# The tail of a two-layer graph kernel: scores of the last group between its value products, an early count of the reciprocals, and three residual adds on GpSimd

## The chip, the cores and the metric

The kernel runs on one core of a Trainium2 chip. The metric is the device time of one launch in microseconds (us), the median of several runs. PE is TensorE, DVE is VectorE, ACT is ScalarE, POOL is GpSimd, SP is SyncE, which issues the writes to memory.

Runs of the same kernel differ by more than the effects studied here: the part of the program ahead of the change took between 1581.35 and 1582.98 us in the profiles below (e4 apart, which changes that part). So, beside the medians, I read from each profile the **tail**: from the start of the scores of batch 123 (the first work that the change touches in earnest) to the end of the instruction that writes the flag.

## The reference, cut to what matters

```python
# layer 0: x is (128 batches, 128 nodes, 512 features)
h = relu(layernorm(x))
x = x + max_over_features(relu(adj @ h + b))           # becomes one number c per batch and node
# layer 1
h = relu(layernorm(x))
q, k, v = h @ Wq + bq, h @ Wk + bk, h @ Wv + bv        # 8 heads of 64
w = softmax(q k^T / 8 + mask(adj == 0))
x = x + w v
```

The softmax is computed without subtracting a maximum: exponentials, times a 0/1 mask, and the row sums come out of the value product through a column of ones in v. At the end the kernel counts how many reciprocals of sums lie in a sane range; if not all do, a general and slower version runs behind it.

## The kernel before

Batches go in groups of four. The products q, k, v of the next group (seven products of eight matmuls each, `p1` to `p7`, for each of q, k, v) are spread over the four batches of the present group, so that TensorE has work while the masks and scalings of a batch run on the other engines. The last group has no next group: only the last product of its own v (`p3`) is left to fill in.

```python
work  = ctx.enter_context(tc.tile_pool(name="work", bufs=2))       # w and o: two buffers each
ps_sc = ctx.enter_context(tc.tile_pool(name="ps_sc", bufs=1, space=PSUM))
ps_av = ctx.enter_context(tc.tile_pool(name="ps_av", bufs=1, space=PSUM))
# ... cut ...
def scores(g, i):          # 16 matmuls over 64 partitions, then two exponentials on ACT
def masks(w):              # two DVE products, both inputs in SBUF
def finish(g, i, w):
    pav = ps_av.tile([P, 2, 512], F32, name="pav")
    # ... 32 matmuls w^T v into 64 partitions each: the "value product" ...
    nc.vector.reciprocal(rs, po[:, :, :, HD])
    o = work.tile([P, 2, 4, HD], F32, name="o")
    nc.vector.tensor_tensor(o, po[:, :, :, 0:HD], rs..., op=ALU.mult)        # scaling, from PSUM
    nc.vector.scalar_tensor_tensor(y, X[g][:, i, :], C[g][:, i : i + 1], y,  # residual
                                   op0=ALU.add, op1=ALU.add)                 # (y is o)
    nc.sync.dma_start(out[b], y)
# ... cut ...
for b in range(B):
    w = scores(g, i)
    for s in range(max(5, len(parts[i]))):
        if s < len(parts[i]):
            parts[i][s]()                  # one product of the next group
        if s == 0:
            masks(w)
        # ... cut: normalisation of later batches ...
    finish(g, i, w)
# behind the loop: two DVE passes over all 1024 reciprocals, a matmul with ones, the flag
```

## Time and profile before

| | before |
|---|---|
| median of 3 runs | 1621.87 us (1621.35 to 1623.84) |
| span of the profile | 1620.0 us |
| start of batch 123's scores to the flag | 1617.21 - 1581.78 = 35.43 us |
| last residual's end to the flag's end | 1617.21 - 1614.91 = 2.30 us |
| flag to the end of the span | 2.79 us |

The prediction below shows the views. The way to read them: the page says which engine bounds the whole (TensorE), and hence that only stretches in which TensorE idles can be shortened by moving other work. The stretches say where those are. The chain says what TensorE waits for there.

### The profile page before, as it was taken

What the parts mean: (1) busy time and instruction counts of PE and PEld (TensorE: products, weight loads), DVE (VectorE), ACT (ScalarE), POOL (GpSimd) and SP (SyncE); (2) the same over time, 40 slices, a digit from 0 to 9 for tenths busy, and PEclk for the clock granted to TensorE, in tenths of its full rate; (3) what the DMA queues carried; (4) which work ended last, traced back from release to release, by engine and by line L of the source; (5) the groups of instructions that cost most, each with busy time, mean ns of one, the idle gap of its engine ahead of it and who ended that gap; (6) DMA issues with size and microseconds to landing.
All of it is one profiled execution on the core that took longest, in us unless ns stands there. A gap on an engine that the chain in (4) does not pass through costs nothing.

```text
span 1620.0 us, 29469 instructions
## 1 busy us (share of the span) xinstructions
PE 1586.6 (98%) x11819; PEld 1319.8 (81%) x11819; DVE 1114.2 (69%) x2044; ACT 422.9 (26%) x844; POOL 259.6 (16%) x278
## 2 busy tenths in 40 slices
PE   6899999999999999999999999999999999999996
PEld 4688888888888888888888888888888888888885
DVE  3576777766777767777767777667777677777655
ACT  2322222222222222222222222222222222222221
POOL 4311111111111111111111111111111111111000
PEclk9999999999999999999999999999999999999999
DMA  4033222232222232222332222322222322223201
GB/s 164 1 72 73 68 60 51 69 75 69 63 46 70 69 79 65 67 44 69 72 73 68 54 56 69 76 68 64 47 69 69 79 65 67 44 69 73 47 27 40
DMA packets 299082, 104.02 MB, mean 64 GB/s; under 512 B 264448, under 2 KB 264576, under 8 KB 298944
## 3 DMA queue, kind: packets, MB, share of 16 engines
q1 hardware_dynamic: 297520, 99.69, 25.5%
q8 instruction: 94, 1.54, 0.4%
q10 hardware_dynamic: 1248, 2.16, 0.4%
q14 instruction: 44, 0.36, 0.1%
q0 software_dynamic: 176, 0.27, 0.1%
HBM read 37.03 MB, written 33.55 MB: 44 GB/s over the span
## 4 chain that ended last, share of the span: by engine, by line
PE 97%; DVE 1%; ACT 1%; issue 0%; DMA 0%; POOL 0%; ACTq 0%; DVEq 0%; POOLq 0%
PE mm L372 72%; PE pav L499 9%; PE sc L477 8%; PE mm L306 6%; PE mm L445 1%; PE pav L306 1%; PE sc L299 0%; DVE w L490 0%; DMA xg<-in_x_dram 0%; ACT hn L272 0%; DVE o L512 0%; DVE o L508 0%; POOL rstd L264 0%; DVE st L259 0%; ACT qT L450 0%
## 5 line engine op out<-in xcount | busy, mean ns | idle before, releaser
L264 POOL TENSOR_TENSOR rstd<-ve,mhalf 128x1 f32<-128x1 f32 x128 | 84.3, 659 | 1225.9 <-DVE ve L262 1087.6
L485 ACT ACTIVATE w<-sc 128x512 f32<-128x512 f32 x256 | 138.9, 595 | 515.4 <-PE sc L477 515.4
L499 PEld LDWEIGHTS pav<-v,w 128*64 128x64 f32 x4096 | 130.3, 137 | 99.6 <-issue 54.4
L372 PE MATMUL mm<-hs,sq_sb 128*128 128x256 f32 x744 | 179.0, 383 | 0.0
L372 PE MATMUL mm<-hs,sk_sb 128*128 128x256 f32 x768 | 176.4, 379 | 0.0
L372 PE MATMUL mm<-sv_sb,hs 128*128 128x256 f32 x768 | 176.2, 379 | 0.0
L273 POOL TENSOR_TENSOR xg<-xg,bv_sb 128x512 f32<-128x512 f32 x128 | 162.9, 1273 | 35.2 <-DVE hn L269 27.5
L490 DVE TENSOR_TENSOR w<-w,live 128x512 f32<-128x512 f32 x256 | 164.7, 685 | 1.0 <-ACT w L485 1.0
L372 PEld LDWEIGHTS mm<-sv_sb,hs 128*128 128x128 f32 x768 | 145.9, 190 | 20.7 <-issue 1.0
L272 ACT ACTIVATE hn<-hn,rstd 128x512 f32<-128x512 f32 x128 | 92.9, 726 | 267.7 <-DVE hn L269 206.3
L372 PEld LDWEIGHTS mm<-hs,sk_sb 128*128 128x128 f32 x768 | 145.9, 190 | 20.3 <-issue 0.5
L372 PEld LDWEIGHTS mm<-hs,sq_sb 128*128 128x128 f32 x744 | 138.8, 190 | 21.4
L499 PE MATMUL pav<-v,w 128*64 128x65 f32 x4096 | 148.5, 224 | 6.7 <-DVE w L490 6.7
L477 PE MATMUL sc<-qT,kT 64*128 64x128 f32 x2048 | 148.7, 285 | 0.0
L420 DVE TENSOR_TENSOR u<-mm,p1b 128x512 f32<-128x512 f32 x63 | 43.5, 691 | 128.3 <-PE mm L372 128.3
L477 PEld LDWEIGHTS sc<-qT,kT 64*128 64x128 f32 x2048 | 124.2, 187 | 9.1 <-issue 0.3
L372 PE MATMUL mm<-hT,wk_sb 128*128 128x256 f32 x512 | 124.2, 385 | 0.0
L372 PE MATMUL mm<-wv_sb,hT 128*128 128x256 f32 x512 | 120.9, 379 | 0.0
L306 PE MATMUL mm<-hn,adjT 128*128 128x512 f32 x236 | 120.5, 592 | 0.0
L372 PE MATMUL mm<-hT,wq_sb 128*128 128x256 f32 x496 | 120.4, 386 | 0.0
L372 PEld LDWEIGHTS mm<-wv_sb,hT 128*128 128x128 f32 x512 | 97.3, 190 | 13.7 <-issue 0.5
L372 PEld LDWEIGHTS mm<-hT,wk_sb 128*128 128x128 f32 x512 | 94.7, 190 | 15.8 <-issue 0.5
(84 smaller groups left out, 2033.1 us busy)
## 6 DMA issues: line engine op xcount, KB each, us to landing
out_dram<-o SPq DMA_DIRECT2D x128, 256.0 KB, 2.1
xg<-in_x_dram SPq DMA_DIRECT2D x62, 512.0 KB, 5.1
hT<-tb SPq DMA_DIRECT2D x960, 32.0 KB, 2.0
xg<-in_x_dram SPq DMA_DIRECT2D x2, 256.0 KB, 3.4
xg<-in_x_dram ACTq DMA_DIRECT2D x2, 256.0 KB, 5.6
wq_sb<-in_L_gnn_Wq_dram SPq DMA_DIRECT2D x1, 512.0 KB, 7.9
wk_sb<-in_L_gnn_Wk_dram SPq DMA_DIRECT2D x1, 512.0 KB, 11.1
wq_sb<-in_L_gnn_Wq_dram ACTq DMA_DIRECT2D x1, 512.0 KB, 10.6
```

The costliest lines, as they stand in the source:

```text
L264: nc.gpsimd.tensor_tensor(rstd, ve, mhalf, op=ALU.pow)
L272: nc.scalar.activation(HN[m], HN[m], AF.Copy, scale=RSTD[m])
L273: nc.gpsimd.tensor_tensor(X[g][:, i, :], X[g][:, i, :], bv_sb, op=ALU.add)
L306: nc.tensor.matmul(pa, adjT, HN[m], start=True, stop=True)
L372: nc.tensor.matmul(bank[:, r, :], lhs, rhs, start=first and r == 0 and c == 0, stop=r == 1 and c == 1, skip_group_check=True,)
L420: nc.vector.tensor_tensor(self.u3, self.b, self.pf[1], op=ALU.add)
L445: nc.tensor.matmul(bank[:, r, :], W["q"][:, c, k * P : (k + 1) * P], h[:, :, c], start=r == 0 and c == 0, stop=r == 1 and c == NC - 1, ski ...
L477: nc.tensor.matmul(psc[:, j, f, :], KT[g][r, f, i * D : (i + 1) * D], QT[g][r, f, i * D : (i + 1) * D], start=True, stop=True,)
L485: nc.scalar.activation(w[:, j], psc[:, j], AF.Exp, scale=HD ** -0.5)
L490: nc.vector.tensor_tensor(w[:, j], w[:, j], live_h, op=ALU.mult)
L499: nc.tensor.matmul(pav[r, h // 4, (h % 4) * HE : (h % 4 + 1) * HE], w[:, h % 2, h // 2, r], V[g % 2][:, i, h, :], start=True, stop=True,)
```

## The change

Its intent is to keep TensorE fed in the last group. The v of the last group is built during batch 123 anyhow; the new order puts the scores of batches 124 to 127 between those products, so that exponentials and masks run early. Two spare places for the weights are the idle `tb` tiles; one value product goes to the idle score bank. The count is split, and three residuals leave DVE: ACT adds c to x, GpSimd adds the result to the scaled output.

```diff
+def spare_tile():
+    t = proj.tile([P, NQ, 2, NC, Q], F32, name="tb")
+    return t.rearrange("p a i c r -> p (a i c r)")
 # ... cut: scores(g, i, spare=False): with spare, its weights go to a tb tile ...
-def finish(g, i, w):
+def finish(g, i, w, spare=False, eng=nc.vector):
     # ... cut: with spare, the value product goes to ps_sc ...
-    nc.vector.scalar_tensor_tensor(y, X[g][:, i, :], C[g][:, i : i + 1], y, op0=ALU.add, op1=ALU.add)
+    if eng is nc.vector:
+        eng.scalar_tensor_tensor(y, x_b, c_b, y, op0=ALU.add, op1=ALU.add)
+    else:
+        nc.scalar.activation(x_b, x_b, AF.Identity, bias=c_b)
+        eng.tensor_tensor(y, x_b, y, op=ALU.add)
-for b in range(B):
+for b in range(B - G - 1):
     # ... cut ...
+        elif s == 3 and b == B - 2 * G + 1:
+            count(0, B - 2 * G)
 # ... cut: the whole count at the end removed ...
+w = scores(g - 1, G - 1)
+k3()
+masks(w)
+v6()
+w0 = scores(g, 0)
+v2()
+masks(w0)
+finish(g - 1, G - 1, w)
+v7()
+w1 = scores(g, 1)
+v5()
+masks(w1)
+w2 = scores(g, 2, spare=True)
+v4()
+masks(w2)
+w3 = scores(g, 3, spare=True)
+finish(g, 0, w0, eng=nc.gpsimd)
+PR[g][2].p3()
+masks(w3)
+finish(g, 1, w1, eng=nc.gpsimd)
+finish(g, 2, w2, spare=True, eng=nc.gpsimd)
+finish(g, 3, w3)
+count(B - 2 * G, B)
```

More of the change, by code (lines that the diff above doesn't have):

```diff
@@ L208, in fast @@
         ps_av = ctx.enter_context(tc.tile_pool(name="ps_av", bufs=1, space=PSUM))
+        CNT = []
         X, HN, TB, HT, HB, QT, KT, C, AMAX, WA, RSTD, MV, PR = ({} for _ in range(13))
@@ L469, in products, with scores @@
             )
-        def scores(g, i):
+        def spare_tile():
+            t = proj.tile([P, NQ, 2, NC, Q], F32, name="tb")
+            return t.rearrange("p a i c r -> p (a i c r)")
+        def scores(g, i, spare=False):
             psc = ps_sc.tile([P, 2, NC, D], F32, name="sc")
@@ L482, in scores @@
                     )
-            w = work.tile([P, 2, NC, D], F32, name="w")
+            if spare:
+                w = spare_tile().rearrange("p (j f d) -> p j f d", j=2, f=NC)
+            else:
+                w = work.tile([P, 2, NC, D], F32, name="w")
             for j in range(2):
@@ L490, in masks @@
                 nc.vector.tensor_tensor(w[:, j], w[:, j], live_h, op=ALU.mult)
-        def finish(g, i, w):
+        def finish(g, i, w, spare=False, eng=nc.vector):
             b = g * G + i
-            pav = ps_av.tile([P, 2, 512], F32, name="pav")
+            if spare:
+                pav = ps_sc.tile([P, 2, NC, D], F32, name="sc").rearrange("p j f d -> p j (f d)")
+            else:
+                pav = ps_av.tile([P, 2, 512], F32, name="pav")
             for h in range(H):
@@ L511, in finish, with count @@
             y = o.rearrange("p k h d -> p (k h d)")
+            x_b, c_b = X[g][:, i, :], C[g][:, i : i + 1]
+            if eng is nc.vector:
+                eng.scalar_tensor_tensor(y, x_b, c_b, y, op0=ALU.add, op1=ALU.add)
+            else:
+                nc.scalar.activation(x_b, x_b, AF.Identity, bias=c_b)
+                eng.tensor_tensor(y, x_b, y, op=ALU.add)
+            nc.sync.dma_start(out[b], y)
+        def count(b0, b1):
+            r = RS[:, b0:b1].rearrange("p b h -> p (b h)")
+            ok = (spare_tile() if b0 == 0 else live)[:, 0 : (b1 - b0) * H]
+            cnt = const.tile([P, 1], F32, name=f"cnt{len(CNT)}")
+            CNT.append(cnt)
+            nc.vector.tensor_single_scalar(ok, r, SUM_LO, op=ALU.is_ge)
             nc.vector.scalar_tensor_tensor(
-                y, X[g][:, i, :], C[g][:, i : i + 1], y, op0=ALU.add, op1=ALU.add
+                ok, r, SUM_HI, ok, op0=ALU.is_le, op1=ALU.mult, accum_out=cnt
             )
-            nc.sync.dma_start(out[b], y)
         with tc.manual_schedule():
@@ L582, in fast @@
                     move(m)
-            ok = work.tile([P, 2, NC, D], F32, name="w").rearrange("p j f d -> p (j f d)")
-            cnt = stat.tile([P, 1], F32, name="cnt")
-            rs_all = RS.rearrange("p b h -> p (b h)")
-            nc.vector.tensor_single_scalar(ok, rs_all, SUM_LO, op=ALU.is_ge)
-            nc.vector.scalar_tensor_tensor(
-                ok, rs_all, SUM_HI, ok, op0=ALU.is_le, op1=ALU.mult, accum_out=cnt
-            )
+            g = NG - 1
+            k3, v6, v2, v7, v5, v4 = parts[G - 1]
+            w = scores(g - 1, G - 1)
[21 more added lines that the diff above has]
+            count(B - 2 * G, B)
             pc = ps_mm.tile([P, 512], F32, name="mm")
-            nc.tensor.matmul(pc[0:1, 0:1], cnt, ones, start=True, stop=True)
+            for k in range(2):
+                nc.tensor.matmul(pc[0:1, 0:1], CNT[k], ones, start=k == 0, stop=k == 1)
             nc.vector.tensor_copy(flag, pc[0:1, 0:1])
```

## The prediction

> **What bounds the kernel now.** I read the page first (engine shares, slices, chain of waits), then the stretches of the last 40 us, the chain piece by piece, the waits and the transfers.
>
> ```profile
> span 1620.0 us, 29469 instructions
> PE 1586.6 (98%) x11819; PEld 1319.8 (81%) x11819; DVE 1114.2 (69%) x2044; ACT 422.9 (26%) x844; POOL 259.6 (16%) x278
> PE 97%; DVE 1%; ACT 1%; issue 0%; DMA 0%; POOL 0%; ACTq 0%; DVEq 0%; POOLq 0%
> ```
>
> TensorE (PE) is busy 98% of the span and holds 97% of the chain. Until the last group it does not wait, so nothing moved off VectorE (DVE) there gains anything. Only the end is open. The stretches (busy us of PE, PEld, DVE, ACT, POOL, each with a count):
>
> ```profile
> 1581.85:1593.49 11.64, 11.64 (x66) 10.00 (x68) 5.52 (x9) 1.67 (x3) 0.00 (x0) 1.00 0.06 24
> 1593.49:1597.63 4.14, 4.10 (x57) 3.36 (x56) 2.34 (x4) 1.08 (x2) 0.00 (x0) 1.00 0.08 32
> 1597.63:1613.12 15.49, 8.77 (x176) 7.41 (x176) 10.52 (x18) 3.26 (x6) 0.00 (x0) 1.00 0.16 61
> 1613.12:1617.21 4.09, 0.19 (x2) 0.09 (x2) 3.63 (x7) 0.00 (x0) 0.00 (x0) 0.52 0.17 64
> 1617.21:1620.00 2.79, 0.00 (x0) 0.00 (x0) 0.00 (x0) 0.00 (x0) 0.00 (x0) 0.50 0.03 9
> ```
>
> Up to 1597.63 PE is full. Then come four batches in which it works 8.77 of 15.49 us, a close of 4.09 us on DVE, and 2.79 us of branch and shutdown. One of those batches in the chain (start, length, what):
>
> ```profile
> 1603.73 1.06 PE pav L499 x28
> 1604.79 0.02 issue
> 1604.82 0.22 DVE RS L506
> 1605.04 0.02 issue
> 1605.06 0.70 DVE o L508
> ...
> 1605.86 0.75 DVE o L512
> 1606.61 1.24 DVE w L490 x2
> 1607.84 0.04 issue
> 1607.89 1.06 PE pav L499 x28
> ```
>
> Period 4.16 us: the value product waits for the masks of its own batch, and the masks stand on DVE behind the reciprocal, the scaling and the residual of the batch before. The scores were ready early. So this is a matter of order, not of work: DVE is busy only 2.88 us per period.
>
> **What the Trainium skill says.** "PSUM — Partial Sum Buffer", section "The four PSUM rules": GpSimd cannot touch PSUM. The diff agrees: scaling from PSUM stays on DVE and only the residual add moves; no row of this trace could contradict it. "GPSIMD Engine Reference", section 3.1: a two-input fp32 add costs GpSimd 1.96 times VectorE's time. The trace agrees nearly: 1273 ns (L273) against 685 ns (L490), 1.86 times. "SBUF — State Buffer", section "Who interferes with whom": a VectorE instruction with two SBUF inputs and a GpSimd one that reads SBUF exclude each other, the later blocked until the earlier ends. The trace of before shows it:
>
> ```profile
> 1496.00 0.69 DVE L420 TENSOR_TENSOR u<-mm,p1a 128x512 f32<-128x512 f32 x1
> 1496.07 1.28 POOL L273 TENSOR_TENSOR xg<-xg,bv_sb 128x512 f32<-128x512 f32 x1
> 1496.61 1.28 DVE L324 TENSOR_TENSOR hs<-hT 128x512 f32<-128x512 f32 x1
> ```
>
> The PSUM-fed add is untouched at 0.69, but the two-SBUF difference takes 1.28 instead of its median 0.684: it ends 0.54 after GpSimd does. In the new tail the masks and the last residual are such instructions; scaling and product adds (one input in PSUM) are not.
>
> **The change part by part.** Durations are from the timeline before. Eight matmuls of a product take PE 1.73, its reader starts 0.23 later; scores 1.09, value product 1.08. DVE: product add 0.69 (the next starts after 0.61), a pair of masks 1.28 (next after 1.20), reciprocal 0.21 (0.25 to the scaling), scaling 0.69, residual 0.75. ACT: a pair of exponentials 1.09, an add over 128x512 about 0.73 (L272 has 726 ns). GpSimd add 1.27.
>
> (a) Nothing leaves PE but small things. The work from 1581.85 on (scores of batch 123) is 7 products x 1.73 + 5 scores x 1.09 + 5 value products x 1.08 = 12.1 + 5.45 + 5.4 = 23.0 us, so a PE without waits would end at 1604.8; today it ends at 1613.10. The most that order can give is 8.3 us.
>
> (b) Scores between products. I laid the new order against these durations by hand. Scores of 124 at 1586.4, of 125 at 1592.0, of 126 at 1594.9, of 127 at 1597.7; each set of exponentials has left the score buffer before the next scores, and PE runs without a gap. The value product of 124 starts at 1598.77 (its last v add ends about 1598.6, so a margin of 0.15), the last product 1599.85 to 1601.6, value products of 125 and 126 at 1601.6 and 1602.7.
>
> (c) DVE after that is the limit: add of the last product 1601.82, masks of 127 until 1603.7, reciprocal and scaling of 125 from 1603.64 to 1604.58. The value product of 127 has to take 125's accumulator, so it runs 1604.61 to 1605.7 (PE loses about 0.9 us here). Scaling of 126 until 1605.56, reciprocal of 127 until 1605.95.
>
> (d) Residuals on GpSimd take 0.75 from DVE three times, but make them later. The sum for 125 runs on GpSimd from 4.58+0.12 to about 1605.97, and its write to memory lands 2.0 to 2.1 us after issue:
>
> ```profile
> out_dram<-o SPq DMA_DIRECT2D x9, 256.0 KB, 2.0
> DMA to landing us min/median/max: 2.0/2.0/2.1
> ```
>
> that is at 1608.1. The output tile has only two buffers (the pool still says bufs=2), so the scaling of 127 reuses 125's buffer and must wait for that landing: 1608.14 instead of 1605.99, **2.15 us of new wait**, the largest term against the change. The ACT adds of x and c lie beside it and cost nothing.
>
> (e) The close: scaling of 127 1608.14 to 1608.83, residual on DVE 1608.92 to 1609.67. GpSimd's last sum ended at 1607.24, so no blocking is left there.
>
> (f) Count split. The part over 120 batches (960 columns: about 0.64+1.15+0.08 = 1.9 us by L588 and L589) goes into batch 121, behind the add at 1568.14, where DVE then idles 0.96, 0.40 and, some 4 us on, 1.72 us: hidden. It delays one product add by about 0.95 us, which no matmul awaits at once. The rest, 64 columns, costs fixed time: about 0.22 + 0.15 + 0.08, two tiny matmuls 0.3, gaps 0.1, the cast 0.15 = 1.0 us from 1609.6. Flag at about 1610.6. Before, from the end of the last residual (1614.91) to the flag took 2.30 us; now about 0.9.
>
> Sum: flag from 1617.21 to 1610.6 = 6.6 us earlier; the 2.79 behind it stay. Span about 1613.4, and time 1621.87 - 6.6 = **1615.3 us**, 0.41% less.
>
> **The rivals.**
> One: order works and the buffer wait does not matter (the scaling is not held, or the write lands in time). Then residual of 127 collides with GpSimd's last sum (1605.97 to 1607.24), ends near 1607.85, flag near 1608.8: 8.4 us saved, 1613.4. For it: in all of the trace before, no DVE row names this write as releaser. Against it: there the buffer returned 8.3 us (two periods) after its scaling, here the need comes 1.4 us after.
> Two: the write of the last batch sets the end. It lands at about 1609.7+2.1 = 1611.8; the shutdown's semaphores began 1.3 us after the flag before (1618.5), so in the new kernel at 1611.9. It just hides. If two writes together take longer than 2.1 us or GpSimd starts late, add 0.5 to 1.5 us: 1616 to 1617.
> Three: the early count or the spare buffers stall PE in the middle: at worst the 1.9 us: 1617.2. Against it speaks the room of (f), and that the last move from these spare buffers was issued four batches earlier.
> Four: DVE, not order, bounds the tail. It has about 17 us of work beside PE's 23.0, so not as a sum; only locally, as in (c).
>
> **Range and chances.** I hold to the buffer wait as the likeliest and give it two parts of three. The range takes rival one at its low side, and rivals two and three at the high side: 1612.9 to 1617.4. The whole of the open end is 8.3 us on PE plus 1.4 in the close, together under 10 us, while 2% is 32.4 us; no way to get faster by 2% exists here, and slower by 2% needs a stall of 32 us that nothing suggests. Faster 0.01, same 0.98, slower 0.01.
>
> **What would show it.** Right: PE full until about 1603.7; value products of 124 to 127 no longer waiting on masks except the last; scaling of 127 with idle time of about 2 us before it, released by a write; flag 0.9 us after the last residual; batch 121 with no PE idle. Wrong: the wait before the last scaling absent (rival one); the last write in the chain behind the flag (rival two); PE idle near 1570 (rival three); masks of 127 lengthened by GpSimd's sum of 124, or the value product of 124 waiting for its v add, each of which would shift all behind it.

## The result, and the profile after

The changed kernel takes 1615.97 us (median of 4 runs, 1615.74 to 1616.53) against 1621.74 us for the kernel before (4 runs). The ratio is 0.9962 with a 95% interval of 0.9945 to 0.998: faster, by far less than 2%. A ratio here is the mean time of one kernel's runs over that of the other's of the same rounds, so not quite the ratio of the medians.

The span in the profile of the changed kernel, and its stretches, cut where the last product ends, where the last reciprocal starts and where the flag is written (columns as in the prediction: stretch, length, busy time of PE, PEld, DVE, ACT, POOL with counts, granted clock, transfers):

```profile
span 1614.1 us, 29483 instructions
```

```profile
1581.52:1602.50 20.98, 20.98 (x206) 17.11 (x204) 12.45 (x21) 7.84 (x14) 0.82 (x1) 1.00 0.07 26
1602.50:1606.59 4.09, 3.20 (x98) 3.00 (x98) 3.50 (x7) 0.00 (x0) 1.65 (x2) 1.00 0.20 70
1606.59:1611.09 4.50, 0.28 (x4) 0.09 (x2) 2.12 (x7) 0.00 (x0) 1.29 (x2) 0.72 0.31 117
```

TensorE is full through the last product, idles 0.89 us among the value products, and is done by 1606.6; the four half-empty periods are gone. What is left is 4.50 us at the end, and in these DVE, too, works only 2.12. The chain says what the end waits for:

```profile
1604.57 0.69 DVE o L520
...
1605.39 1.28 POOL o L529
1606.67 0.02 issue
1606.69 2.01 DMA out_dram<-o
...
1608.82 0.70 DVE o L520
1609.52 0.03 issue
1609.55 0.75 DVE o L526
```

The scaling of 125 (1604.57), GpSimd's sum of 125, its write to memory, and only then the scaling of 127 (1608.82), in the same buffer. In the list of waits (who, for whom, total, times, longest) a write now holds DVE, which it never did before:

```profile
DVE o L520 <- DMA out_dram<-o: 2.4, 2, 2.0
```

The two are 0.37 us ahead of the scaling of 126 and 2.02 us ahead of that of 127. The first cost nothing: the reciprocal of 127 waited for its value product anyhow, and started 1.33 us after the end of the scaling of 125; in e1 below, where both waits are gone, it started 1.34 us after it.

### The profile page after: what moved, and what is told of

Read it like the earlier page. It is cut to its first block, busy times and chain, and to the rows that moved or that the text cites. A ratio compares the mean times of both kernels' runs of the same rounds, so it can differ in the third digit from the quotient of the medians.

```text
span 1614.1 us, 29483 instructions
## 1 busy us (share of the span) xinstructions
PE 1585.8 (98%) x11821; PEld 1318.7 (82%) x11821; DVE 1111.7 (69%) x2044; ACT 425.0 (26%) x847; POOL 263.7 (16%) x281
## 4 chain that ended last, share of the span: by engine, by line
PE 97%; DVE 1%; ACT 1%; POOL 0%; issue 0%; DMA 0%; ACTq 0%; DVEq 0%; POOLq 0%
PE mm L373 72%; PE sc L483 9%; PE pav L511 8%; PE mm L307 6%; PE mm L446 1%; PE pav L307 1%; PE sc L300 0%; POOL rstd L265 0%; DMA xg<-in_x_dram 0%; ACT hn L273 0%; POOL xg L274 0%; DVE st L260 0%; DMA out_dram<-o 0%; ACT qT L451 0%; DVE o L520 0%
```

## The experiments

Eleven runs followed, one of them the changed kernel again; all gave correct results. The tails, with what each is:

| run | what differs | median us | ratio to before | tail us |
|---|---|---|---|---|
| before | | 1621.74 | | 35.43 |
| changed | | 1615.97 | 0.9962 | 29.57 |
| e9 | changed, again | 1616.65 | 0.9956 | 29.59 |
| e6 | order alone | 1617.42 | 0.9972 | 30.58 |
| e5 | count alone | 1622.08 | 1.0002 | 34.29 |
| e2 | order and count, residuals on DVE | 1615.72 | 0.9959 | 29.09 |
| e3 | GpSimd residuals alone | 1625.26 | 1.002 | 37.78 |
| e1 | changed, free output buffers | 1614.41 | 0.9955 | 27.72 |
| e7 | e1, last masks first | 1614.88 | 0.9954 | 27.96 |
| e10 | e1, one change of block kind less | 1613.90 | 0.9941 | 27.53 |
| e11 | e10, last masks first, GpSimd held back | 1613.71 | 0.9941 | 27.02 |

(e8 moves the flag itself and e4 is about the steady part; they are told below.) e1 to e8 ran on one chip, where the kernel before had a median of 1622.11 us, e9 to e11 on another, where it had 1623.16; medians are compared only within such a group. The intervals of the ratios are some 0.0015 wide to each side, 2.4 us. So the times alone show that the changed kernel is faster than the one before, but hardly how the variants rank; that is read from the tails, with one profile for each variant.

**e1: is the wait for the write real?** The outputs of batches 126 and 127 go to idle tiles of the normalised input.

```diff
-o = work.tile([P, 2, 4, HD], F32, name="o")
+if g == NG - 1 and i >= 2:
+    o = proj.tile([P, N], F32, name="hn").rearrange("p (k h d) -> p k h d", k=2, h=4)
+else:
+    o = work.tile([P, 2, 4, HD], F32, name="o")
```

> The changed kernel, but the scaled outputs of batches 126 and 127 get a third and fourth buffer (idle tiles of the normalised input), so that neither scaling waits for a write to memory. Theory (buffer wait): the 0.37 us before the scaling of 126 and the 2.02 us before that of 127 go; the last residual then meets GpSimd's sum of 126 (ends near 1607.9 on the changed kernel's clock) and is held by it a little, ends near 1608.5 instead of 1610.30; span 1612.3, 1.8 us under the 1614.1 of the changed kernel. Rival (the wait was hidden by something that ends as late, such as the last write or GpSimd's queue): span stays within 0.4 us of 1614.1.

Span 1612.4, tail 27.72: 1.85 us less than changed, as the theory had it; the rival falls. No write is left among what DVE waits for. The last residual does meet GpSimd's sum of 126, in the timeline of this run (start, length, engine, line, operation):

```profile
1606.77 1.26 POOL L532 TENSOR_TENSOR hn<-xg,hn 128x512 f32<-128x512 f32 x1
1607.78 0.80 DVE L529 SCALAR_TENSOR_TENSOR hn<-xg,c,hn 128x512 f32<-128x512 f32 x1
```

GpSimd ends at 1608.03, DVE at 1608.58: the residual is held by only 0.05 us (0.80 against 0.75).

**e2: what do the GpSimd residuals bring?** The three `eng=nc.gpsimd` are removed.

> The changed kernel with all four residuals of the last group on VectorE again (two output buffers as before). Theory: the GpSimd sum of 125 takes 1.27 us plus 0.13 us to start where VectorE takes 0.75, and with the same two buffers the write of 125 sets the last scaling; so without GpSimd the last scaling starts about 0.5 us earlier, and the span is 0.4 to 0.5 us SHORTER than 1614.1, about 1613.6. Rival (moving residuals off VectorE is what it says, a relief of the busiest engine of the tail): three times 0.75 us come back on VectorE, span longer by 1 to 2 us, 1615 to 1616.

The tail is 29.09, which is 0.48 us shorter than with GpSimd, and the wait ahead of the last scaling shrinks from 2.02 to 0.33 us:

```profile
1609.72 0.69 DVE L520 TENSOR_TENSOR o<-pav,RS 128x512 f32<-128x512 f32 x1 [0.33 <-DMA out_dram<-o]
```

So with two output buffers this part of the change costs 0.48 us on net. This does not carry over to the free buffers of e1. Residuals on DVE with free buffers were not run, but an estimate can be made from e2: without its wait of 0.33 us its tail would be 28.76, about 1.0 us more than the 27.72 of e1. (The span in this profile, 1615.1, is longer than the changed kernel's; its tail merely began 1.46 us later. This is why the tail is used. The medians, 1615.72 and 1615.97, cannot tell.)

**e6 and e5: the other two parts alone.** e6 is the new order with the residuals on DVE and the whole count at the end; e5 is the kernel before with the split count.

> The changed kernel with residuals on VectorE and the whole count at the end: the new order alone. Theory (the parts add up): 1.5 us more than the run with VectorE residuals, so 30.6 us from the start of batch 123's scores to the flag, against 35.43 before and 29.57 on the changed kernel; span about 1615.2. Rival (the order only pays together with the other parts): more than 32 us from those scores to the flag.

> The kernel before with the split count alone (120 batches counted in batch 121, 8 at the end). Theory: the close from the end of the last residual to the flag shrinks from 2.30 to 0.79 us as on the changed kernel, and the early part is hidden, TensorE having no idle time in batches 121 to 123: span 1.5 us shorter than 1620.0, 1618.5. Rivals: the early part holds the product adds and TensorE (idle time near 1570, gain under 0.5 us); or the last write sets the end, then the gain is smaller and the span ends a constant time after that write lands.

e6: tail 30.58, predicted 30.6. So the order is worth 35.43 - 30.58 = 4.85 us, the count on top of it 30.58 - 29.09 = 1.49, GpSimd on top of both minus 0.48: together the 5.86 us of the tails. (About 0.2 us of what the count gains is lost again behind the flag; see "The rest" below.)

e5: the close from the last residual to the flag is 0.81 us instead of 2.30, as expected, and the matmuls around batch 121 run on without a gap. But the tail shrank by 1.14 only, since one of the four periods took 4.50 us instead of 4.16: a residual started 0.36 us late, and the profile names no releaser for it. The median, 1622.08 beside 1622.11, shows no gain at all; the runs of this kernel lay between 1620.77 and 1624.38, which is more than the effect. Part of this goes with the granted clock: three of its six runs had a mean clock below 0.998, and four of the ten of the kernel before. The runs at 0.998 alone have a mean of 1621.35 (three) against 1621.87 (six), a gain of 0.5 us. Too few to be sure; the rest is open.

**e3: the GpSimd residuals without the new order.**

```diff
-finish(g, i, w)
+finish(g, i, w, eng=nc.gpsimd if B - G <= b < B - 1 else nc.vector)
```

> The kernel before with only the residuals of batches 124 to 126 on GpSimd. Theory (exclusive SBUF reads): the masks, with two SBUF inputs, meet the GpSimd sum that starts 0.13 us after the scaling; the first mask of the next batch is held until GpSimd is nearly done and takes about 1.2 us instead of 0.69; each of three periods grows from 4.16 to about 4.6 us, span about 1.4 us LONGER than 1620.0. Rival (no exclusion): the masks start when the exponentials are ready, which was within 0.1 us of when VectorE was free; periods 4.05 to 4.16, span 0 to 0.4 us shorter.

The tail is 2.35 us longer than before, more than expected. The first two periods took 4.62 us instead of 4.16, because the masks of the next batch were held:

```profile
1601.86 1.27 POOL L517 TENSOR_TENSOR o<-xg,o 128x512 f32<-128x512 f32 x1 [79.83 <-DVE o L508]
1602.52 1.76 DVE L490 TENSOR_TENSOR w<-w,live 128x512 f32<-128x512 f32 x2 [0.79 <-ACT w L485]
```

The pair of masks takes 1.76 instead of 1.29. In the third period the masks came late and were not held; there the granted clock of TensorE fell to 0.55 on the mean (1609.92 to 1613.25), and the last scores and value product took 1.85 and 2.30 us instead of 1.16 and 1.38. Before, the clock stayed at 1.00 until 1612. That GpSimd's part led to this I cannot say from one profile. What is shown: taken alone this part makes the kernel slower (ratio 1.002, interval 1.0004 to 1.0035). The hold accounts for 0.92 of the 2.35 us; how the rest divides is open.

**e4: what does a change from products to half-height blocks cost?** The changed kernel's last product started 18.97 us after the scores of 123, and the prediction had said 18.00. In its chain eight matmuls took 1.92 us wherever scores or a value product followed, and sixteen 3.65, once 1.73 and once 1.92:

```profile
1582.68 3.65 PE mm L373 x16
1586.33 1.09 PE sc L483 x16
1587.42 1.92 PE mm L373 x8
1589.35 1.08 PE pav L511 x32
```

To magnify this, the kernel before gets one such change more in every batch:

```diff
-w = scores(g, i)
 for s in range(max(5, len(parts[i]))):
     if s < len(parts[i]):
         parts[i][s]()
     if s == 0:
-        masks(w)
+        w = scores(g, i)
+    if s == 1:
+        masks(w)
```

> The kernel before, but in every batch the scores stand behind the first product instead of directly behind the value product of the batch before: no work added, one more change per batch from full-height products to the half-height score matmuls. Theory: each such change costs TensorE about 0.19 us (in the changed kernel eight matmuls took 1.92 us where a score or value block followed, against 1.73 us where a product followed), which is why the tail came 0.9 us later than predicted: 124 batches x 0.19 = about +23 us, span near 1643. Rival (no cost of the change; the delay in the tail had another cause): span within 2 us of 1620.

The median is 1675.00, 53 us more and not 23: the run was not clean, since the later masks now stood in front of product adds that TensorE waits for. But there are batches without such a wait, and in them the period can be read. First the kernel before, then this run, both from the chain:

```profile
1512.14 1.08 PE pav L499 x32
...
1514.32 8.83 PE mm L372 x40
...
1524.01 1.08 PE pav L499 x32
```

```profile
1004.03 1.08 PE pav L499 x32
1005.11 1.92 PE mm L372 x8
...
1016.09 1.08 PE pav L499 x32
```

The same matmuls in 11.87 and in 12.06 us: 0.19 us for one change. It is no single find: the kernel before has 88 batches with these same matmuls, at 11.86 us, and in this run 57 of the 88 take 12.06. Most of the other 29 us lie in the remaining periods and in those with six products; TensorE's list of waits has 58 waits for the product adds of L411 and L420 there, and none for them in the kernel before.

**e10: one change less.** In e1, the value product of 123 goes directly behind the scores of 124.

```diff
 w0 = scores(g, 0)
+finish(g - 1, G - 1, w)
 v2()
 masks(w0)
-finish(g - 1, G - 1, w)
 v7()
```

> The run with free output buffers, and the value product of 123 directly behind the scores of 124, so one change from products to half-height blocks less. Theory (each such change costs TensorE 0.19 us): everything from the scores of 125 on comes 0.2 us earlier, 27.5 us from batch 123's scores to the flag against 27.72. Rival (no cost): 27.7.

27.53: 0.19 us less, as the theory said. The kernel has a median of 1613.90 and beats both kernels (in the same rounds before took 1623.16 and changed, e9, 1616.65).

**e7, e8: two attempts that failed.** DVE idles 0.98 us waiting for the last product while the masks of 127 could run; e7 puts those masks first.

```diff
-PR[g][2].p3()
 masks(w3)
+PR[g][2].p3()
```

> The run with free output buffers, and the masks of batch 127 ahead of the last product add on VectorE, which idles 0.98 us waiting for that product while the masks could run. Theory (the local limit is VectorE behind the last product): reciprocal of 125 about 0.8 us earlier, and the last residual then meets GpSimd's sum of 126 squarely and is held 0.4 us: 26.9 us from batch 123's scores to the flag against 27.72, span 1611.5. Rival (no exclusion of the residual): 26.5 us. Rival (the last write or GpSimd's queue sets the end): span stays at 1612.4.

Tail 27.96, not 26.9. My expectation had looked at the last residual and overlooked that the masks move on top of GpSimd's sum of 124:

```profile
1602.06 2.37 DVE L499 TENSOR_TENSOR tb<-tb,live 128x512 f32<-128x512 f32 x2
1602.27 1.60 POOL L532 TENSOR_TENSOR o<-xg,o 128x512 f32<-128x512 f32 x1 [80.05 <-DVE o L523]
1604.34 0.68 DVE L394 TENSOR_TENSOR v<-mm,u 128x512 f32<-128x512 f32 x1
```

The first mask came first and GpSimd took 1.60 instead of 1.27; then GpSimd had the turn and the second mask waited. The pair took 2.37 us instead of 1.28, the last product add came at 1604.34, and the gain was gone.

e8 further merges as in e10 and puts the last count and the flag ahead of the last residual.

> As the run with the masks first, and also: the value product of 123 directly behind the scores of 124 (one change from products to half-height blocks less, 0.19 us), and the count of the last group and its flag ahead of the last residual, so that only the residual and its write come last. Theory (shutdown follows the flag by 3.0 us but cannot end sooner than about 1.75 us after the last write lands, as on the changed kernel): the residual ends about 26.2 us after batch 123's scores, its write lands 2.1 us later, span about 1611.3 to 1611.6, so no gain over the run with the masks first although the flag comes 1.2 us earlier. Rival (the write is not waited for): the end follows the flag by 3.0 us, span 1610.2.

It is slower than e1 and e7: median 1617.14. Beside the same hold of the masks, the first pass of the count, 0.19 us of work, fell into GpSimd's sum of 126:

```profile
1608.08 1.26 POOL L536 TENSOR_TENSOR hn<-xg,hn 128x512 f32<-128x512 f32 x1 [0.19 <-PE mm L649]
1608.16 1.24 DVE L545 TENSOR_SCALAR live<-RS 128x64 f32<-128x64 f32 x1
```

So the residual ended 28.2 us after the scores of 123 instead of the 26.2 expected. The run does show that the end waits for the last write. SP's own waits in the shutdown contain

```profile
SPq L689 <- DMA out_dram<-hn: 2.5, 1, 2.5
```

and the span ended 1.4 us after that write landed. In the other profiles, where the flag came last, the span ended 2.8 to 3.0 us after the flag. In this profile the last write took 4.3 us where most take 2.0 to 2.1; why, I don't know. The rival (the write is not waited for) falls.

**e11: masks first, without the clash.** To test the reading of e7, GpSimd gets a tiny instruction ahead of its sum of 124 that reads one column of the masked weights, so that it cannot start before the masks are done.

```diff
+nc.gpsimd.tensor_tensor(t, w3[:, 1, NC - 1, D - 1 : D], ones, op=ALU.mult)   # behind masks(w3)
 # then GpSimd's residual of 124
```

> As the run before it, and the masks of batch 127 ahead of the last product add once more, but GpSimd's residual of 124 held back by a tiny GpSimd instruction that reads the masked weights, so that masks and residual no longer overlap. Theory (in the run with the masks first the pair took 2.37 us instead of 1.28 because GpSimd's sum of 124 and the masks exclude each other): the pair takes 1.28 again, the reciprocal of 125 comes 0.8 us earlier than with the masks behind, and 26.7 us pass from batch 123's scores to the flag, the least of all; the last residual is held some 0.4 us by GpSimd's sum of 126. Rival (the masks took 2.37 us for another reason, such as their place right behind the scaling of 124): the pair stays near 2.4 us and the total above 27.7.

```profile
1601.55 1.28 DVE L499 TENSOR_TENSOR tb<-tb,live 128x512 f32<-128x512 f32 x2
1602.97 0.19 POOL L640 TENSOR_TENSOR ve<-tb,ones 128x1 f32<-128x1 f32 x1 [81.06 <-DVE tb L499]
1603.18 1.27 POOL L534 TENSOR_TENSOR o<-xg,o 128x512 f32<-128x512 f32 x1
```

The pair takes 1.28 again and GpSimd 1.27: it was the clash. The tail is 27.02, the shortest of all, 0.3 us over the expected 26.7: in the chain 0.23 us stand ahead of the scaling of 125 for which the profile names no releaser. The last residual was held by 0.05 us (0.80 against 0.75), not by the expected 0.4. The median, 1613.71, is not told apart from e10's 1613.90.

> The changed kernel itself, timed on the same chip as the two runs beside it: median near 1616, and 29.6 us from batch 123's scores to the flag as in its first profile.

e9 came out as expected (1616.65, tail 29.59).

## Why the prediction was right

It said 1615.3 us, 1612.9 to 1617.4, and 1615.97 came; 6.6 us were to be saved, and 5.77 were. By its steps:

- **The bound and (a).** Right. All of the gain lies behind batch 123, and no part of the change could reach 2%.
- **(b) Scores between products.** Right that TensorE runs without a gap through the last product. The mis-sized term is the 1.73 us for each product: it was the time of a product that another product follows. Ahead of scores or a value product it is 1.92. Five such changes lie in front of the last product, 5 x 0.19 = 0.95, and that product started 0.97 us later than laid out (18.97 against 18.00). e4 and e10 both give 0.19 for one. "TensorEngine Tiling (Array Packing)", section "Key Properties", of the Trainium skill says that changing the tiling mode drains TensorE; the prediction had not looked there. The page has no figure. These traces agree with it in one direction only: the cost appears in going from full products to the half-size blocks. Scores take 1.09 us and a value product 1.08 whether a product or the other kind of block follows, though these tiles differ in shape, too (64x128 and 128x64). So that the 0.19 us are this drain is not shown; what is shown is what one such change costs.
- **(c) DVE after the last product.** Right: TensorE lost 0.89 us there, predicted 0.9.
- **(d) The two output buffers.** Right, and the largest term: 2.02 us ahead of the last scaling, 2.15 predicted. e1 shows that it is real time: without it the tail is 1.85 us shorter. Not foreseen were the 0.37 us ahead of 126's, where 124's write took 2.6 us and not 2.1; they were hidden behind the value product of 127.
- **(e) and (f).** Right: the last residual was not held (0.75 us), the close took 0.79 us against about 0.9, and the early count stopped no matmul.
- **The rest.** On the chain's clock, which the prediction used (scores of 123 at 1581.59, 0.07 us later than in the timeline), the flag came 29.50 us after these scores against 28.75; the 0.75 us are the 0.97 of (b) less small gains in (d) and (f). The shutdown took 3.01 instead of 2.79. TensorE's earlier part was 0.26 us shorter in this profile, by chance, so luck took back a third of the miss. The longer shutdown is no chance: in the packed traces each engine's load of the flag takes 0.73 to 0.84 us in the changed kernel, e1, e2, e5, e7 and e9 to e11, and 0.46 to 0.55 in before, e3, e4 and e6. In these four, which count at the end, the last write had landed before the load; in the others it had not. But in e8, with a write under way as well, the loads took 0.54 to 0.57, so the cause is open.
- **Rival one** (the wait doesn't matter) is refuted by e1. **Rival two** (the last write sets the end) was not reached in the changed kernel, but e8 shows that the mechanism exists. **Rival three** (the early count stalls TensorE) did not happen. **Rival four** holds only locally, as in (c).

What the prediction did not say outright is that the GpSimd part is a loss as long as there are two output buffers. Its step (d) contains it: the sum ends later on GpSimd, hence the write, hence the buffer. e2 measured it as 0.48 us.

## What to carry to other kernels

When work moves to a slower engine to relieve a busy one, follow the result to its next owner: here the slower residual delayed a write, the write held one of two output buffers, and the relieved engine waited for that buffer. With a free buffer the same move may well pay (the estimate at e2). When small work is slipped between large blocks of matmuls, add a price for each change of block kind. And before two engines that exclude each other get more to do at the same time, line up their instructions: a short instruction on the critical path can be held for the whole of a long one that is not.

## What the Trainium skill lacked or had wrong

- "TensorEngine Tiling (Array Packing)", "Key Properties": names the drain on a change of tiling mode but gives no size and no direction. Here: 0.19 us for one change from 128x128 products to the half-height scores (e4: 12.06 against 11.87 us for the same matmuls; e10: tail 0.19 us less), and nothing seen on the way back or between scores and value products.
- "SBUF — State Buffer", "Who interferes with whom": does not say how a hold looks in a profile. Here the held instruction appears early and long, not late (in e3 a pair of masks at 1.76 instead of 1.29; in e8 a `tensor_scalar` of 64 columns at 1.24 instead of 0.19), and no wait for GpSimd is named.
- The same section says, of VectorE's 2-port modes, that the one that issues first has the shared ports for its whole instruction; it doesn't say that a train of short instructions and one long one alternate. In e7 GpSimd got in between two masks, and both sides lost (1.60 instead of 1.27, and 2.37 instead of 1.28).
- "GPSIMD Engine Reference", section 3.1, gives 1.96 times VectorE's time for a two-input add, for 2048 columns only; at 512 columns this kernel shows 1273 ns for GpSimd's add against 685 for VectorE's product of two inputs, 1.86 times.
